# Layer 0's queries join the seven products; row sums kept in DRAM; two norms pinned

## The chip, the cores and the metric

The kernel runs on one core of a Trainium2 chip. A core has a matrix engine (TensorE, PE below; its weight loads are shown as PEld), a vector engine (VectorE, DVE), a scalar engine (ScalarE, ACT), a general-purpose engine (GpSimd, POOL) and a sync engine (SyncE, SP) that here only issues DMAs. The metric is device time in microseconds of one execution; the kernel before takes 2171.02 us, the median of three runs (2167.05 to 2172.69).

## The reference, cut to what matters

Two transformer layers in float32. Layer 0 is attention with 16 heads of 128 on 2048 tokens of width 512 (four sequences of 512), then a mixture of eight experts with two chosen per token; layer 1 is the other way round. The change is in the projections and rotations of layer 0's attention:

```python
q = (hidden_states @ Wq + bq).reshape(Bq, Sq, NH, D).transpose(0, 2, 1, 3)
q = apply_rope(rmsnorm(q, qn_w), pos)
...
ck = apply_rope(rmsnorm(entries @ Wk + bk, kn_w), block_ends)
sc = jnp.einsum('bhsd,bcd->bhsc', q, ck) * scale
...
lk = apply_rope(rmsnorm((hidden_states @ Wlk + blk).reshape(Bq, Sq, NH, D).transpose(0, 2, 1, 3), kn_w), pos)
lv = (hidden_states @ Wlv + blv).reshape(Bq, Sq, NH, D).transpose(0, 2, 1, 3)
```

`apply_rope` turns the first 64 of a head's 128 entries by the token's position and leaves the other 64 alone. `rmsnorm` divides by the root of the mean square and multiplies by a weight vector. Scores against compressed keys `ck` keep the eight largest per token; scores against `lk` are taken in a band of 128 tokens.

## The kernel before, in words

**Steps.** Layer 0's attention is done in 32 steps, one for each pair of heads (a group, `g`) and each sequence (`b`), in the loop at line 822. Step i computes the attention of its pair and, in between, the projections of step i+1, which `project(i+1)` hands over as pieces (lines 828 to 856). The written order within a step is: scores of the first head (`sp`, `st`, lines 600 and 609); queries of the first half of the tokens (`pq`, line 554); first keys; sums of rows; a job of other work (`run0`); scores of the second head; transposes `trs` of the first head's sparse weights (line 635); another job; second keys with the transposes `trq` (line 543) of what is ready; the first context (`ca`, `cb`, `cc`, lines 651 to 657); `trs` of the second head; queries of the second half; a job; the second context; transposes `trc` of the first context (line 677); a job; values; more `trq` and `trc`; the output product `op` (line 685), added to the residual (line 688).

**Jobs.** In the early steps they are layer norms of later sequences, compressed keys and routing; in steps 5 to 24 the experts of layer 0 (`trm`, line 382, then `hp`, line 392, with the weights fetched by POOL one expert ahead, lines 373 and 375); from step 25 on the experts' results are gathered and added, and layer 1's first norms are done.

**Seven products.** Tokens are cut into two halves and the 512 input features into two halves, and the weights for keys and for values are the two column blocks. Instead of eight block products, seven are computed of sums of blocks: p1, p2 (first keys, line 560), p6, p7, p4 (second keys, line 567), p5, p3 (values, line 578). They need sums of token blocks (`x1`, `x2`, `x3`; lines 515 to 518 and 571, DVE, each step) and sums of weight blocks (`combine_weights`, line 96, once per group). Each product is a PSUM bank of two chunks of 256 columns, four matmuls. Queries are computed directly: sixteen matmuls of 256 columns per step (line 550).

**After a product.** DVE adds partial results and biases on the way out of PSUM. `rope` (line 426) takes squares on ACT with a running sum, the power -1/2 on POOL (lines 434 to 437), and rotates on DVE, over all 128 entries of a head since the table `t1` also holds the norm's weight. Queries are then scaled by their norm on ACT (line 447); keys are not, their norm enters as the scale of the exponential (line 613). `trq` turns the result and ACT copies it to `qkT` (line 544), which has two buffers.

**The context.** `context` (line 640) uses three PSUM banks of the tag `sc`, which has three buffers; the second head's context takes the same three. They are free when DVE has read the sums (line 660), ACT has scaled the sparse half (line 668) and DVE has added both (line 670). Products, queries, `hp` and `op` share the tag `mm` with three banks, transposes the tag `tr` with two.

**Who orders the instructions.** The kernel is written as one program; a planner gives each engine a fixed order ahead of time. It goes by program order, but when by its own estimate an instruction could not start yet it takes a later one that could. Instructions wrapped in `keep_in_program_order` keep their written order among each other. On the chip each engine works through its list, and each queue of DMAs (SP's, ACT's and POOL's) through its own.

**The start.** SP loads the first token tile, `Wq` and the biases, then the second tile, `Wlk`, the norm vectors, the rotation tables, two more tiles, and `Wlv` (lines 119 to 139). `tables` (line 175) makes `t1` and `t2` on POOL from them. `layernorm` (line 197) takes statistics on DVE, the power on POOL and the result on DVE, then four transposes `trx`.

## Time and profile before

| | |
|---|---|
| median of three runs | 2171.02 us |
| the profiled execution | 2168.7 us |
| its span, first to last instruction | 2166.8 us |
| layer 0's attention loop | about 61 to 1500 us |
| layer 1 | about 1500 to 2167 us |
| PE busy | 2108.3 us, 97% of the span |
| PEld busy | 1392.0 us, 64% |
| DVE busy | 1458.9 us, 67% |
| ACT busy | 848.4 us, 39% |
| POOL busy | 687.0 us, 32% |
| DMA, mean over the span | 97 GB/s |

An engine's busy time is the union of its instructions. Matmul records overlap (their ends are modelled), so the time that a stream of matmuls takes is read from one start to the next. A float32 matmul is recorded as two instructions. The chain of work that ended last has PE with 68% of the span, DVE 8%, POOL 5%, DMA 3%, ACT 3%; 13% are issue. Its largest lines are 524 (the seven products, 15%), 554 (queries, 9%) and 685 (output product, 9%).

### The profile page before, as it was taken

The numbers are of one execution on the slowest core, as the hardware profiler recorded it, in microseconds if no ns is written. First come the engines' busy times: TensorE is split into PE (matmuls) and PEld (weight loads), VectorE is DVE, ScalarE is ACT, GpSimd is POOL, SyncE is SP. The second block draws the span as 40 slices with busy tenths as digits, with TensorE's granted clock in tenths as the row PEclk, the third lists the DMA queues.
The fourth block names the chain that finished last, engine by engine and source line by source line (L and its number), as shares of the span: only waits on it lengthen the run. The fifth ranks groups of instructions, "written<-read, shape, count | busy, mean of one in ns | idle before, by whom it ended". The sixth has DMA issues, their size and how long they took to land.

```text
span 2166.8 us, 28936 instructions
## 1 busy us (share of the span) xinstructions
PE 2108.3 (97%) x9970; PEld 1392.0 (64%) x9970; DVE 1458.9 (67%) x3674; ACT 848.4 (39%) x2649; POOL 687.0 (32%) x725
## 2 busy tenths in 40 slices
PE   6999999999999999999999999999999999999998
PEld 5667877777777777777777887885334343443332
DVE  6868976666666766666666788885485444446775
ACT  3444444334444334444433444552333233333332
POOL 3212234343323323333323444443012222213430
PEclk9999999999999999999999999999999999999998
DMA  7001023322322332232232112102016566653321
GB/s 229 35 11 38 11 73 97 106 78 83 105 98 74 105 105 71 83 124 80 78 123 83 59 50 63 35 30 92 10 69 209 203 227 209 205 198 117 107 83 41
DMA packets 70813, 211.24 MB, mean 97 GB/s; under 512 B 8449, under 2 KB 25857, under 8 KB 60673
## 3 DMA queue, kind: packets, MB, share of 16 engines
q0 software_dynamic: 22592, 139.47, 19.2%
q1 hardware_dynamic: 45760, 65.63, 9.4%
q10 hardware_dynamic: 2304, 4.20, 0.5%
q8 instruction: 81, 1.33, 0.3%
q14 instruction: 76, 0.61, 0.1%
HBM read 176.24 MB, written 33.03 MB: 97 GB/s over the span
## 4 chain that ended last, share of the span: by engine, by line
PE 68%; issue 13%; DVE 8%; POOL 5%; DMA 3%; ACT 3%; SPq 0%; POOLq 0%; ACTq 0%; DVEq 0%
PE p L524 15%; PE pq L554 9%; PE op L685 9%; PE hp_r L392 7%; PE st L609 4%; PE sp L600 2%; PE trq L543 2%; PE qp L905 2%; POOL we_r L375 2%; PE ca L653 2%; PE o L976 1%; DVE pS L936 1%; PE st L916 1%; DMA row_r<-yd,slot_r 1%; PE cc L657 1%
## 5 line engine op out<-in xcount | busy, mean ns | idle before, releaser
L392 PE MATMUL hp_r<-we_r,xT_r 128*128 128x512 f32 x624 | 283.4, 597 | 4.3 <-DMA we_r<-in_ewx,wrow_r 4.2
L617 POOL TENSOR_TENSOR lT<-lT,lmask 128x512 f32<-128x512 f32 (+1 forms) x128 | 151.2, 1196 | 318.6 <-ACT lT L613 318.6
L554 PE MATMUL pq<-Wq,xnT 128*128 128x256 f32 x1024 | 234.0, 381 | 1.2 <-DVE u L570 1.2
L685 PE MATMUL op<-Wo,cT 128*128 128x512 f32 x512 | 230.5, 599 | 2.1 <-DVE lv L587 2.1
L554 PEld LDWEIGHTS pq<-Wq,xnT 128*128 128x128 f32 x1024 | 190.2, 191 | 24.9 <-DVE u L570 1.5
L392 PEld LDWEIGHTS hp_r<-we_r,xT_r 128*128 128x128 f32 x624 | 115.1, 191 | 139.4 <-issue 129.6
L373 POOL DMA_INDIRECT xr_r<-xnd,rows_r x78 | 83.6, 1072 | 330.9 <-PE trm_r L382 232.9
L613 ACT ACTIVATE lT<-st,ss 128x256 f32<-128x256 f32 (+1 forms) x256 | 96.8, 443 | 234.2 <-PE st L609 234.1
L544 ACT COPY qkT<-trq 128x512 f32<-128x512 f32 x128 | 74.7, 583 | 231.6 <-PE trq L543 231.2
L685 PEld LDWEIGHTS op<-Wo,cT 128*128 128x128 f32 x512 | 91.7, 190 | 113.8 <-issue 82.3
L918 ACT ACTIVATE pT<-st 128x1024 f32<-128x1024 f32 x128 | 123.8, 1019 | 70.1 <-PE st L916 54.5
L437 POOL TENSOR_TENSOR ss<-ss,nhalf 128x4 f32<-128x4 f32 x128 | 144.5, 1129 | 10.7
L384 ACT COPY xT_r<-trm_r 128x512 f32<-128x512 f32 x78 | 45.2, 580 | 260.6 <-PE trm_r L382 203.0
L688 DVE TENSOR_TENSOR acc<-acc,op 128x512 f32<-128x512 f32 x128 | 87.5, 684 | 80.7 <-PE op L685 80.5
L394 DVE TENSOR_TENSOR yr_r<-hp_r,we_r 128x512 f32<-128x512 f32 x78 | 53.7, 688 | 116.5 <-PE hp_r L392 116.5
L447 ACT ACTIVATE r<-r,ss 128x128 f32<-128x128 f32 x256 | 81.9, 390 | 105.8 <-POOL ss L437 103.4
L524 PE MATMUL p<-Wlv,x 128*128 128x256 f32 x512 | 117.5, 380 | 0.0
L524 PE MATMUL p<-Wlk,xnT 128*128 128x256 f32 x512 | 117.4, 383 | 0.0
L524 PE MATMUL p<-wT,x 128*128 128x256 f32 x512 | 117.4, 380 | 0.0
L407 POOL DMA_INDIRECT row_r<-yd,slot_r x64 | 75.3, 1176 | 120.1 <-DVE row_r L1008 53.6
L524 PEld LDWEIGHTS p<-wT,x 128*128 128x128 f32 x512 | 95.9, 190 | 23.8 <-issue 12.1
L524 PEld LDWEIGHTS p<-Wlv,x 128*128 128x128 f32 x512 | 95.5, 190 | 20.7 <-issue 9.1
(253 smaller groups left out, 4394.4 us busy)
## 6 DMA issues: line engine op xcount, KB each, us to landing
yd<-yr_r SPq DMA_DIRECT2D x78, 256.0 KB, 2.4
acc<-in_x SPq DMA_DIRECT2D x16, 256.0 KB, 5.1
Wq<-in_Wq SPq DMA_DIRECT2D x8, 512.0 KB, 3.7
Wlk<-in_Wlk SPq DMA_DIRECT2D x8, 512.0 KB, 3.6
xnd<-xn ACTq DMA_DIRECT2D x16, 256.0 KB, 2.6
Wlv<-in_Wlv SPq DMA_DIRECT2D x8, 512.0 KB, 9.1
Wo<-in_Wo SPq DMA_DIRECT2D x8, 512.0 KB, 3.6
xnd<-xn SPq DMA_DIRECT2D x16, 256.0 KB, 2.0
```

The costliest lines, as they stand in the source:

```text
L373: G.indirect_dma_start(out=x, out_offset=None, in_=xnd, in_offset=at_rows(self.r.rows[:, i : i + 1]))
L392: PE.matmul(hp, lhsT=xT[:, k, :], rhs=w[:, ts(k, HID)], start=(k == 0), stop=(k == KC - 1))
L437: G.tensor_tensor(ss, ss, nhalf[:, 0:n], ALU.pow)
L447: A.activation(r1[:, h, :], r1[:, h, :], AF.Copy, scale=ss[:, h : h + 1])
L524: PE.matmul(p[:, c, :], lhsT=x[:, k, ts(c, P)], rhs=w[:, k, :], start=(k == 0), stop=(k == 1))
L554: PE.matmul(pq[:, c, :], lhsT=xnT[:, k, ds(b * S + (2 * t + c) * P, P)], rhs=w_q[:, k, :], start=(k == 0), stop=(k == KC - 1))
L609: PE.matmul(st[:, ds((t % 2) * 256, n)], lhsT=qkT[:, HG + h, ts(t, P)], rhs=qkT[:, h, ds(t * P, n)], start=True, stop=True)
L613: A.activation(lT[:, ds(half * 512 + c * 256, n)], st[:, ds(c * 256, n)], AF.Exp, scale=norm_k[(i, half)][:, c * HG + h : c * HG + h + 1])
L617: G.tensor_tensor(dst, dst, lmask.rearrange("p a w j -> p (a w j)")[:, 0:n], ALU.mult)
L685: PE.matmul(op, lhsT=cT[:, h, ts(t, P)], rhs=wo[:, h, :], start=(h == 0), stop=(h == HG - 1))
L688: V.tensor_tensor(acc[:, n, :], acc[:, n, :], op, ALU.add)
L918: A.activation(pt[:, ts(pair, 2), :], st, AF.Exp, scale=SCALE1)
```

## The change

The two column blocks of the seven products are no longer keys and values. Block A is now the pair's queries (256 columns) and the first head's keys (128); block B is the pair's values (256) and the second head's keys (128). The host lays the weights and biases out so (`wA`, `wB`, `bA`, `bB`). Each product has 384 columns and is made in two chunks, each with a PSUM bank and an eviction of its own. The separate query matmuls are gone.

With that: all of block A for the first half of the tokens comes out of `first` (p1, p2), for the second half out of `second` (p6, p7, p4), block B out of `third` (p5, p3). Keys of the first head are turned by `turn_keys(0)` late in the step, those of the second head, which stand in `lv` beside the values, by `turn_keys(1)` in the next step, after its first scores. `qkT` has one buffer. The rotation covers the 64 entries that turn and is done in place; what the norm weights do to the other 64 goes into a vector `turned` that scales keys on their copy out of PSUM. Tables have 64 entries for three heads, and the compressed keys have tables of their own.

The four sums of rows are computed in the first four projections only and written to DRAM (`xsd`); the later ones load them on SP. The first two token tiles are loaded ahead of the weights, the weights come in halves, and the statistics and results of the first two layer norms are pinned to program order. A constant that nothing used is dropped.

```diff
     def load_group(g, between=None):
...
+        b2 = wpool.tile([P, 2, 3 * D], F32, tag="b2", name=f"b2_{g}")
         ws = []
+        for i, nm in enumerate(("wA", "wB")):
+            w = wpool.tile([P, KC, 3 * D], F32, tag=nm, name=f"{nm}_{g}")
+            for f in range(2):
+                nc.sync.dma_start(out=w[:, ts(f, 2), :],
+                                  in_=a[nm][g, ts(f, 2 * P), :].rearrange("(k p) c -> p k c", p=P))
+                if between:
+                    between(nm, f)
+            nc.sync.dma_start(out=b2[:, i, :], in_=a["b" + nm[1]][g].partition_broadcast(P))
             ws.append(w)
...
+    def load_between(nm, f):
+        if nm == "wA" and f == 1:
+            for w, src in enumerate(("qn_w", "kn_w")):
+                nc.sync.dma_start(out=nw[:, w, :], in_=a[src].partition_broadcast(P))
+                nc.sync.dma_start(out=wcol[:, w : w + 1], in_=a[src].rearrange("(d o) -> d o", o=1))
+            nc.sync.dma_start(out=cos, in_=a["c_cos"][:, :, 0:R])
             nc.sync.dma_start(out=sin, in_=a["c_sin"])
             for n in range(2, TC):
                 load_x(n)
     load_x(0)
+    load_x(1)
     groups = {0: load_group(0, load_between)}
...
     def layernorm(n, pool, bank):
+        pin = tc.keep_in_program_order if n < 2 else (lambda x: x)
         st = small.tile([P, 6], F32, tag="st", name=f"st_{n}")
-        V.bn_stats(st, acc[:, n, :])
+        pin(V.bn_stats(st, acc[:, n, :]))
...
-        V.tensor_scalar(xn, acc[:, n, :], mv[:, 0:1], mv[:, 1:2], ALU.subtract, ALU.mult)
+        pin(V.tensor_scalar(xn, acc[:, n, :], mv[:, 0:1], mv[:, 1:2], ALU.subtract, ALU.mult))
...
+    def rotate(x, tt1, tt2, n, pool, name):
...
+        V.tensor_tensor(r1, x[:, :, 0:R], tt1, ALU.mult)
+        V.tensor_tensor(r2[:, :, 0:32], x[:, :, 32:R], tt2[:, :, 0:32], ALU.mult)
+        V.tensor_tensor(r2[:, :, 32:R], x[:, :, 0:32], tt2[:, :, 32:R], ALU.mult)
+        V.tensor_tensor(x[:, :, 0:R], r1, r2, ALU.add)
...
+    def load_sums(i):
+        for n in range(4):
+            xs[n] = wk0.tile([P, 2, 256], F32, tag=f"x{n}", name=f"x{n}_{i}", bufs=1)
+            if i >= B:
+                nc.sync.dma_start(out=xs[n].rearrange("p k t -> p (k t)"), in_=xsd[steps[i][1], n])
...
+        def product(nm, x, w, c):
+            p = psum("mm", f"{nm}_{i}_{c}")[:, 0 : 3 * D]
+            for k in range(2):
+                PE.matmul(p, lhsT=x[:, k, ts(c, P)], rhs=w[:, k, :], start=(k == 0), stop=(k == 1))
+            return p
...
+        def finish(t):
+            x = qb[t].rearrange("p c (h d) -> p (c h) d", d=D)
+            sq[t] = squares(x, 6, wk0, f"{i}_{t}", float(D))
...
+            rotate(x, by(t1), by(t2), 6, wk0, f"{i}_{t}")
+            for j in (0, 1, 3, 4):
+                A.activation(x[:, j, :], x[:, j, :], AF.Copy, scale=sq[t][:, j : j + 1])
...
+        def second(between):
+            u2, u3 = u["u2"], tmp("u3")
             t2_, t3_, t4_ = sums_w[g]
+            for c in range(2):
+                V.tensor_tensor(u2[:, c, :], product("p6", xs1, t2_, c), u2[:, c, :], ALU.add)
+                V.tensor_tensor(u3[:, c, :], product("p7", xs2, t3_, c), u2[:, c, :], ALU.add)
             between()
+            qb[1] = wk0.tile(rows3, F32, tag="qb", name=f"qb1_{i}")
+            for c in range(2):
+                V.tensor_tensor(qb[1][:, c, :], u3[:, c, :], product("p4", x22, t4_, c), ALU.subtract)
+            finish(1)
+        def third():
+            u2, u3 = u["u2"], u["u3"]
+            u5 = wk0.tile(rows3, F32, tag="qb", name=f"u5_{i}")
+            by_head = lambda x: x.rearrange("p c (h d) -> p c h d", d=D)
+            for c in range(2):
+                V.tensor_tensor(u5[:, c, :], product("p5", xs0, w_b[:, 0:2, :], c), b2[:, 1, :], ALU.add)
+            V.tensor_tensor(lv[:, 2:4, :, 0:D], by_head(u3), by_head(u5), ALU.add)
+            V.tensor_tensor(u2, u2, u5, ALU.add)
+            for c in range(2):
+                p3 = product("p3", xs3, w_b[:, 2:4, :], c).rearrange("p (h d) -> p h d", d=D)
+                V.tensor_tensor(lv[:, c, :, 0:D], p3, by_head(u2)[:, c], ALU.add)
+            x = lv[:, :, 2, 0:D]
+            ss = squares(x, TC, wk0, f"{i}_k", float(D))
+            rotate(x, t1[:, :, 2, :], t2[:, :, 2, :], TC, wk0, f"{i}_k")
...
     for i, (g, b) in enumerate(steps):
...
+        em0, lT0 = scores(i, 0, now)
+        turn_last(1)
+        if more:
+            load_sums(i + 1)
+            qkT, sums_x, first, second, third, turn_queries, turn_keys = project(i + 1)
+            first()
+            sums_x()
         run0((i, 0))
+        em1, lT1 = scores(i, 1, now)
         sT0 = turn(i, 0, em0)
         run0((i, 1))
-        back_k1 = keys_b(back_q0)
-        back_k0()
+        if more:
+            second(lambda: turn_queries(0))
         ctx0 = context(i, 0, lT0, sT0, lv)
         sT1 = turn(i, 1, em1)
-        back_q1 = queries_b()
         if b == 2 and g + 1 in groups:
             combine_weights(g + 1)
         run0((i, 2))
-        back_k1()
         ctx1 = context(i, 1, lT1, sT1, lv)
         turn_context(i, 0, ctx0, cT)
+        if more:
+            turn_queries(1)
         run0((i, 3))
-        values_()
-        back_q1()
+        if more:
+            turn_keys(0)
+            third()
         turn_context(i, 1, ctx1, cT)
```

## The prediction

> **What bounds the kernel now.** I read the slices first, then busy time by stage, then the timeline of one step engine by engine, then the waits of TensorE (PE), and the start last. The slices say PE is busy to nine tenths and at full clock from the second slice on. The stages say how hard that is: layer 0 has 32 steps, and a step with expert work is

> ```profile
> core 0: us, PE busy (x) PEld busy (x) DVE busy (x) ACT busy (x) POOL busy (x), PEclk, DMA share, GB/s
> 61.16:110.86 49.70, 46.13 (x249) 34.21 (x248) 38.81 (x120) 21.11 (x73) 13.84 (x20) 1.00 0.07 27
> 849.81:896.79 46.98, 46.98 (x237) 36.25 (x237) 30.36 (x84) 19.60 (x73) 14.65 (x16) 1.00 0.23 79
> 1267.00:1308.00 41.00, 40.10 (x217) 32.83 (x218) 36.13 (x93) 18.86 (x70) 18.45 (x20) 1.00 0.15 44
> ```

> (columns after the stretch: length, then busy us and instructions per engine.) From 520 to 1179 us PE waits for nobody; the steps repeat at 46.98 us. In the early steps and in steps 25 to 30 PE stands idle for up to 3.6 us per step. So in layer 0 PE's own work sets the time, and VectorE (DVE, 30 of 47), ScalarE (ACT, 20), GpSimd (POOL, 15) and the DMAs have slack. The same step on PE:

> ```profile
> 849.64 7.17 PE L685 MATMUL op<-Wo,cT 128*128 128x512 f32 x16
> 856.65 1.05 PE L600 MATMUL sp<-ckT,qkT 128*128 128x32 f32 x8
> 859.06 3.62 PE L554 MATMUL pq<-Wq,xnT 128*128 128x256 f32 x16
> 862.51 3.62 PE L524 MATMUL p<-Wlk,xnT 128*128 128x256 f32 x16
> ...
> 869.25 3.60 PE L392 MATMUL hp_r<-we_r,xT_r 128*128 128x512 f32 x8
> 872.69 3.62 PE L524 MATMUL p<-wT,x 128*128 128x256 f32 x16
> ...
> 880.75 0.61 PE L657 MATMUL cc<-cv,sT 128*128 128x129 f32 x4
> 881.20 0.60 PE L635 MATMUL trs<-ident,s 128*32 128x128 f32 x4
> 881.64 3.62 PE L554 MATMUL pq<-Wq,xnT 128*128 128x256 f32 x16
> 885.09 0.60 PE L382 MATMUL trm_r<-ident,xr_r 128*128 128x128 f32 x4
> 885.97 0.39 PE L653 MATMUL ca<-lv,lT 128*128 128x129 f32 x2
> ```

> Start to start is what counts. A matmul stands as two records. Sixteen records of 256 columns take 3.454 us (859.06 to 862.51 and on): 0.2159 each. Eight of 512 take 3.44 (869.25 to 872.69): 0.430; the sixteen of line 685 take 7.01: 0.438.

> **The matmuls.** Per projection, before: queries 32 records and seven products of 8, in all 88 x 0.2159 = 19.00 us. After: seven products x 2 halves x 2 chunks x 2 records = 56 records of 384 columns, a shape the trace lacks. Halfway between 0.2159 and 0.430 it costs 0.323, halfway to 0.438 it costs 0.327; I take 0.3235, nearest to the back-to-back rows. 56 x 0.3235 = 18.12, so **0.88 us less** (0.69 to 0.91). Transposes stay at 16 per step. Over 32 projections: **-28 us** (-22 to -29).

> [...] The rows show 0.84 ns per column at 256 and at 512 alike, so the rows decide and give nothing beyond the columns.

> **Evictions, rotation, row sums.** DVE rows: 0.69 us for 512 columns, 0.415 for 256, 0.283 for 128; by that line 384 is 0.55 and 768 about 0.95. Before, a projection takes 11 x 0.69 + four row sums x 0.68 + four rotations x 1.67 = 17.0 us. After: 14 x 0.55 + 2 x 0.95 = 9.6, two rotations of 384 and 192 columns (1.8 each) and one of 256 and 128 (1.4): 14.6, plus 2.7 while the sums are still made (the first four projections). DVE is not the bound in a 46.98 us step, so the 2.4 us are worth nothing there; without that cover they are worth 2.4. ACT keeps 16 squares, 8 scalings and 4 copies; POOL has three norm pairs instead of four. Products now come every 1.29 us against 0.55 of eviction, and three banks let PE run two ahead: the top-k of the first scores holds DVE until 862.35, PE needs the first bank back at 863.4, 0.5 us of room.

> **Sums from DRAM.** 28 steps load four tiles of 256 KB and four write them. Loads of that size land in 2.7 us (the xa rows of layer 1), four one after another 11 us. Their buffers come free when the products of the step before have read them, p3 as the last at about 849; p6 wants them at about 871. Even if all four are issued only then, they have 21 us. The wait they add stands on SP; behind it are the expert rows' writes (2.4 us to land) and the next group's weights, neither wanted for 14 us. Four issues at 0.43 us (SP's rows) are 1.7 us of SP. Price: 0; if all cover went, up to 11 us a step, which nothing in the trace points to. The expert weights land 6.4 us after their issue and have 14.9 us in the new order (16.2 now).

> **What is late next: the second context.** This is the step I trust least. Its banks are those of the first context, which are free only after sums, ACT's halves and DVE's last multiply-add. Today the second half of the queries (3.46 us, 881.64) lies between. It is gone: after 'cc' there is only trs 0.44 and trm 0.44 in steps 5 to 24, trs alone in most others. Now the engines that free the banks:

> ```profile
> 881.40 0.16 DVE L660 TENSOR_SCALAR sums<-cc 128x2 f32<-128x2 f32 x1 [0.28 <-PE cc L657]
> 882.82 0.86 DVE L670 SCALAR_TENSOR_TENSOR ctx<-ca,sums,half 128x128 f32<-128x128 f32 x3
> ```

> 'cc' ends at 881.2, 'ca' is free at 883.7: 2.5 us. PE would come after 0.88: a hole of **1.6 us**, if ACT takes the halves at once. For the second context it does not:

> ```profile
> 888.07 0.19 ACT L432 ACTIVATION_READ_ACCUMULATOR sq<-qb_q 128x1 f32 x1
> 889.74 1.28 ACT L447 ACTIVATE r<-r,ss 128x128 f32<-128x128 f32 x4 [1.48 <-POOL ss L437]
> 890.92 0.60 ACT L668 ACTIVATE half<-cb,sums 128x128 f32<-128x128 f32 x2
> ```

> The halves were ready at 889.0 and stood 1.9 us behind the scaling of the queries, which waited for POOL's power (1.04 us). Nobody noticed, for 7 us of matmuls followed. In the changed kernel the second half's queries come out of p4, right ahead of the first context: eviction 0.55, three squares 1.3, POOL 1.5, scaling 1.28 puts the scaling at about 3.7 us after p4 and the halves behind it at 5.0, 'ca' free 4.4 us after 'cc': a hole of 3.5 us. Against it: the order on PE is not strictly the written one. At 285 to 295 us op, trc, sp and st are interleaved record by record, so the planner fills holes that it sees, and p5 (2.59 us) needs only its row sum and a bank. What it does not see is POOL's delay: the wait 'PE trck <- ACT r_ck' (1.7 us, 1.7, 0.4) is such a case. Bounds per step: 0 (all filled) and 1.9 (3.5 less 1.6 filled). I take **0.45**, nearer to zero because in steady steps PE now shows no hole at all: x 31 = **+14 us** (0 to +59).

> **The start.**
> ```profile
> 11.34 2.11 PE L210 MATMUL trx<-ident,xn 128*128 128x128 f32 x8 [11.34 <-DVE xn L206]
> 13.32 5.09 PE L554 MATMUL pq<-Wq,xnT 128*128 128x256 f32 x16
> 21.75 0.66 PE L210 MATMUL trx<-ident,xn 128*128 128x128 f32 x4 [3.34 <-DVE mv L203]
> ```
> The first norm's result waited on DVE behind the second tile's statistics, which waited for its load (sixth in SP's queue, there at 9.7 us). Now x0 and x1 load first and the norms are pinned, so 'xn' can be done at about 6.0 (power at 5.37 plus 0.55), 5.3 us sooner. But the bias of the first products is queued behind both halves of the weights, the norm vectors, cos, sin and two tiles, 2.2 MB; at the first slice's 229 GB/s plus 2.9 us to land it comes at 12 to 15, against the first eviction at 23.55 today. From 23 to 61 DVE is full, so the gain ends between nothing and 9 us. Tables on POOL: 12 operations instead of 6, about 5.7 us against 5.2 (640 elements 1.58, 160 about 0.5), still ahead of the third and fourth norm's power. I take **-4** (-9 to +2).

> The new columns of single floats (two loads, 4 bytes per partition) resemble the 'part' load, which landed in 2.9 us, so I charge nothing. [...]

> **Sum.** -28 + 14 - 4 = -18 on the profiled execution, 2168.7 (span 2166.8 and 1.9 around it): 2150.7. The median of the three, 2171.0, lies 2.3 above: **2153**.

> **Rivals.** About 0.3% (6.5 us) is what a measurement of this kernel can tell from no change.
> (1) *All holes filled*: -28 - 6 = 2137. For it: interleaving at 285 us, no hole in steady steps. Against: planned times that POOL misses.
> (2) *The second context waits*: place, line 653's first matmul; price 1.9 a step. 31 x (1.9 - 0.88) = +32, less 4 + 1 for the start and the projection ahead of the loop: about 2198, **slower**. It decides from 0.88 us per step on. For it: 890.92 above. Against: p5 is ready.
> (3) *Saving given back*: hole of 0.7 to 1.1, 2165 to 2177, no change. The lower cover in steps 25 to 30 would do it there alone (today 4.9 us from the end of the second context to its transposes).
> (4) *Row sums late*: p6 waits on a load. Slower; against it the 11 us of four loads within 21.

> **Chances.** Forecast 0.37 (2145 to 2164), (1) 0.27, (2) 0.20, (3) 0.14, (4) 0.02. Faster 0.64, same 0.14, slower 0.22. The range for 8 in 10 takes in (1) and the lower part of (2): 2136 to 2186; the forecast's own is 2145 to 2164.

> **What would show it.** Right: a steady step near 46.5 us, records of 384 columns 0.32 apart, p5 ahead of the second 'ca', first transposes at 6 to 7 us. The hole shows as idle before 'ca' with DVE ctx or ACT as releaser. Wrong: 384 columns at over 0.34; PE waits for x or for 'u' evictions; steps over 46.98.

## The result, and the profile after

The changed kernel takes 2271.04 us (median of four, 2267.98 to 2271.81) against 2170.1 for the kernel before (median of four, 2167.05 to 2172.69): ratio 1.0463, 95% interval 1.0445 to 1.0481. It is **slower by 4.6%**, and the prediction was wrong in direction and range. The profiled execution spans 2269.7 us (2166.8 before) at a mean granted clock of 0.977 (0.993).

Stretches of the changed kernel first, an early step, a steady one and a late one, then two pieces inside the steady step (columns: length, then busy us and instructions of each engine, granted clock, DMA):

```profile
core 0: us, PE busy (x) PEld busy (x) DVE busy (x) ACT busy (x) POOL busy (x), PEclk, DMA share, GB/s
112.52:162.90 50.38, 48.34 (x231) 31.18 (x229) 37.49 (x107) 23.42 (x81) 11.51 (x12) 1.00 0.09 32
856.10:906.97 50.87, 47.79 (x206) 31.98 (x205) 29.87 (x80) 20.17 (x72) 14.52 (x14) 0.97 0.30 104
1306.52:1352.90 46.38, 41.69 (x182) 28.67 (x180) 30.61 (x87) 19.32 (x70) 17.63 (x18) 0.93 0.24 69
882.93:886.01 3.08, 0.00 (x2) 0.03 (x1) 0.50 (x2) 2.32 (x9) 1.80 (x2) 1.00 0.14 31
886.01:890.62 4.61, 4.61 (x27) 4.61 (x28) 1.23 (x7) 1.00 (x4) 0.00 (x0) 0.63 0.12 42
```

The steady step was 46.98 us with TensorE busy throughout. Now it is 50.87, TensorE stands idle for 3.08 of them, and in the 4.61 us behind the idle the mean granted clock is 0.63: for 3.41 us of them, from 886.88 on, TensorE runs at half clock (0.5). The same step on TensorE:

```profile
859.38 5.33 PE L538 MATMUL p<-wA,xnT 128*128 128x384 f32 x16
864.54 0.60 PE L392 MATMUL trm_r<-ident,xr_r 128*128 128x128 f32 x4
...
881.89 0.60 PE L650 MATMUL trs<-ident,s 128*32 128x128 f32 x4
882.33 0.60 PE L392 MATMUL trm_r<-ident,xr_r 128*128 128x128 f32 x4
886.01 0.46 PE L668 MATMUL ca<-lv,lT 128*128 128x129 f32 x2 [3.08 <-DVE ctx L685]
886.30 0.39 PE L666 MATMUL ca<-lv,lT 128*128 128x129 f32 x2
...
887.49 0.64 PE L666 MATMUL cb<-lv,lT 128*128 128x129 f32 x2
889.21 1.07 PE L672 MATMUL cc<-cv,sT 128*128 128x129 f32 x4
```

Sixteen records of 384 columns go from 859.38 to 864.54: 0.3225 each. Between the contexts stand trs and trm and nothing else, and `ca` of the second context waits. From 887.05 the same two-record pieces that took 0.22 us start to start take 0.43, until 890.3. What `ca` waited for, on GpSimd (POOL), ScalarE (ACT) and VectorE (DVE), in the timelines of the same step:

```profile
881.67 0.56 POOL L443 TENSOR_SCALAR ss<-ss 128x6 f32<-128x6 f32 x1 [8.16 <-ACT sq L442]
882.31 1.35 POOL L444 TENSOR_TENSOR ss<-ss,nhalf 128x6 f32<-128x6 f32 x1
...
883.69 1.28 ACT L552 ACTIVATE qb<-qb,ss 128x128 f32<-128x128 f32 x4 [2.12 <-POOL ss L444]
884.88 0.60 ACT L683 ACTIVATE half<-cb,sums 128x128 f32<-128x128 f32 x2
...
882.33 0.20 DVE L678 RECIPROCAL sums<-sums 128x8 f32<-128x8 f32 x1
885.51 0.35 DVE L685 SCALAR_TENSOR_TENSOR ctx<-cb,sums,half 128x128 f32<-128x128 f32 x1 [2.98 <-ACT half L683]
885.78 0.86 DVE L685 SCALAR_TENSOR_TENSOR ctx<-ca,sums,half 128x128 f32<-128x128 f32 x3
```

The halves (ScalarE's scaled copies of a context's sparse half) need only the reciprocal, done at 882.5. They start at 884.88, for on ScalarE's queue the scaling of the second half's queries stands ahead of them and waits for GpSimd's power until 883.69. The waits of TensorE over the whole execution (us in total, times, longest):

```profile
PE ca L668 <- DVE ctx L685: 68.6, 26, 3.4
PE p L538 <- DVE u L578: 14.6, 6, 3.3
PE trx L220 <- DVE xn L216: 12.7, 4, 5.9
...
PE trg_r L236 <- ACT lr_r L231: 4.1, 1, 4.1
```

Layer 0 carries all of it. Step by step (ends of line 700's matmuls, line 685 before), changed less before: +5.7 us in step 0, -0.1 in steps 1 to 4, **+70.7 in steps 5 to 23**, **+26.8 in steps 24 to 30**, +0.6 in step 31, and -0.9 in layer 1, whose code is the same.

Steps 5 to 23 are accounted for: 19 x (3.08 - 0.88) = 41.8 from the idle less the saved matmuls, and 16 stretches of 3.41 us at half clock, each taken at half its length, 1.7 (50.87 less 49.22 makes 1.65): 27.3. That is 69.1 of 70.7; the rest is that step 5 took only 45.2 before. A step takes 50.87 where the half clock follows its idle, and 49.22 where it does not (steps 8, 13, 18).

### The profile page after: what moved, and what is told of

It reads as the page before. It is cut to its first block, busy times and chain, and to the rows that moved or that the text cites. A ratio compares the mean times of both kernels' runs of the same rounds, so it can differ in the third digit from the quotient of the medians.

```text
span 2269.7 us, 27315 instructions
## 1 busy us (share of the span) xinstructions
PE 2120.4 (93%) x8946; PEld 1234.2 (54%) x8946; DVE 1444.4 (64%) x3596; ACT 867.5 (38%) x2649; POOL 673.8 (30%) x667
## 4 chain that ended last, share of the span: by engine, by line
PE 60%; issue 13%; DVE 9%; POOL 7%; ACT 6%; DMA 4%; SPq 0%; POOLq 0%; ACTq 0%; DVEq 0%
PE p L538 20%; PE op L700 10%; PE hp_r L402 6%; ACT sq L442 3%; PE st L624 3%; PE sp L615 2%; PE qp L922 2%; POOL ss L444 2%; DMA row_r<-yd,slot_r 2%; POOL we_r L385 2%; PE o L993 1%; ACT qb L552 1%; PE ca L668 1%; PE st L933 1%; DMA we_r<-in_ewx,wrow_r 1%
## 5 line engine op out<-in xcount | busy, mean ns | idle before, releaser
L538 PE MATMUL p<-wT,x 128*128 128x384 f32 x512 | 175.6, 493 | 4.5 <-DVE u L578 3.8
L538 PE MATMUL p<-wB,x 128*128 128x384 f32 x512 | 177.1, 489 | 0.3 <-DVE u L591 0.3
L538 PE MATMUL p<-wA,xnT 128*128 128x384 f32 x512 | 173.4, 491 | 2.2 <-DVE u L570 2.2
L442 ACT ACTIVATE sq<-qb 128x128 f32<-128x128 f32 x384 | 119.0, 310 | 125.4 <-DVE qb L583 57.7
L668 PE MATMUL ca<-lv,lT 128*128 128x129 f32 x384 | 83.4, 302 | 69.1 <-DVE ctx L685 68.6
L538 PEld LDWEIGHTS p<-wA,xnT 128*128 128x128 f32 x512 | 95.5, 192 | 63.6 <-DVE u L570 3.4
L443 POOL TENSOR_SCALAR ss<-ss 128x6 f32<-128x6 f32 x64 | 34.9, 546 | 291.2 <-ACT sq L442 291.2
L538 PEld LDWEIGHTS p<-wB,x 128*128 128x128 f32 x512 | 92.6, 191 | 52.3 <-DVE u L591 1.3
L552 ACT ACTIVATE qb<-qb,ss 128x128 f32<-128x128 f32 x256 | 81.8, 390 | 98.9 <-POOL ss L444 95.1
L628 ACT ACTIVATE lT<-st,ss 128x256 f32<-128x256 f32 (+1 forms) x128 | 47.1, 448 | 176.6 <-PE st L624 176.6
```

Of the source, the lines that this page charges most:

```text
L442: A.activation(sq, x[:, h, :], AF.Square, accum_out=ss[:, h : h + 1])
L538: PE.matmul(p, lhsT=x[:, k, ts(c, P)], rhs=w[:, k, :], start=(k == 0), stop=(k == 1))
L552: A.activation(x[:, j, :], x[:, j, :], AF.Copy, scale=sq[t][:, j : j + 1])
L668: PE.matmul(loc[t], lhsT=lT[:, ds(t * 256, P)], rhs=lv[:, t, h, :], start=(t == 0), stop=True)
```

## The experiments

Layer 1, untouched by every run, took between 664.2 and 672.1 us in the profiled executions, one of each kernel, with 19.5 to 33.7 us of it at half clock. The start varies too: in the changed kernel and the seven others that share its start, step 0's first scores come at 65.2 to 69.0 us. So a difference of a few us in a total says little; the lengths of like steps of layer 0 repeat to some 0.02 us within an execution, and they decide.

**The halves first.** Is the idle made by ScalarE's order? The last line below calls the scaling for t = 1, each instruction pinned in program order.

```diff
-            for j in (0, 1, 3, 4):
-                A.activation(x[:, j, :], x[:, j, :], AF.Copy, scale=sq[t][:, j : j + 1])
+            if t == 0 or i == 0:
+                scale(t, lambda ins: ins)
...
         ctx0 = context(i, 0, lT0, sT0, lv)
+        if more:
+            scale_last[i + 1]()
```

> Edit: the changed kernel with one thing moved: ScalarE's scaling of the second half's query rows (line 552, t = 1) comes behind the two copies of halves (line 683) of the first context, where it stood ahead of them and waited for GpSimd's power. Theory (the hole ahead of the second context is the scaling's wait for GpSimd, 2.3 us of the 3.1, and only an idle of that length is followed by 3.4 us of half clock): the first context's ca is read 0.4 us after its halves, at about 883.9 instead of 885.9 in the step at 856 us, the idle ahead of the second context falls to 1.2 to 1.6 us, no half clock follows it, and a step of 5 to 23 takes 47.3 to 47.8 us instead of 49.2 to 50.9: 2180 to 2195 us in all. Rival A (the hole is the bank itself and the chain of halves, sums and reciprocal, whatever ScalarE's order): the idle stays near 3 us and the time at 2270. Rival B (the half clock has another cause than the idle): the idle falls but the stretches at half clock stay, 2205 to 2220 us.

Measured: 2179.73 us (ratio to before 1.0051, 1.0033 to 1.0069), 91 us less than the changed kernel. Its timelines of VectorE (the reciprocal), ScalarE, VectorE again and TensorE in a steady step:

```profile
833.51 0.20 DVE L684 RECIPROCAL sums<-sums 128x8 f32<-128x8 f32 x1
...
833.81 0.62 ACT L689 ACTIVATE half<-cb,sums 128x128 f32<-128x128 f32 x2 [1.06 <-DVE sums L684]
834.33 0.62 ACT L689 ACTIVATE half<-cc,sums 128x128 f32<-128x128 f32 x2
834.87 1.28 ACT L557 ACTIVATE qb<-qb,ss 128x128 f32<-128x128 f32 x4
...
834.74 0.86 DVE L691 SCALAR_TENSOR_TENSOR ctx<-ca,sums,half 128x128 f32<-128x128 f32 x3
...
833.52 0.60 PE L392 MATMUL trm_r<-ident,xr_r 128*128 128x128 f32 x4
834.97 0.46 PE L674 MATMUL ca<-lv,lT 128*128 128x129 f32 x2 [0.85 <-POOL ss L444]
```

The halves start 0.1 us after the reciprocal (833.51 and 0.20), the idle is 0.85 us, no stretch at half clock is left in steps 5 to 23, and each from step 6 on takes 47.00 (step 5 46.5). The idle is shorter than the 1.2 to 1.6 expected, and so are the steps, and the total is 0.3 us under its band; both rivals fall. (The releaser printed for `ca`, GpSimd's power, frees no bank; in the code the bank comes free with the multiply-adds on VectorE, 834.74 here, so a printed releaser is checked against the timeline.) The matmuls' saving shows here too: 46.98 - 0.88 + 0.85 = 46.95.

**Work in the hole.** The idle stays where it is made, and ready matmuls are put into it.

```diff
-        run0((i, 1))
+        expert = 5 <= i < 24
+        if not expert:
+            run0((i, 1))
...
         sT1 = turn(i, 1, em1)
-        run0((i, 2))
+        run0((i, 1) if expert else (i, 2))
```

> Edit: the changed kernel in which, in steps 5 to 23, the first piece of the expert's products (3.4 us of matmuls that wait for nothing of this step) is emitted between the turn of the first context and the second context instead of ahead of it, and the two later pieces one place later each; ScalarE's order is as it was. Theory (TensorE is idle there only because the planner has nothing that is ready, and the half clock follows from the idle): the wait ahead of the second context disappears in those 19 steps, no stretch at half clock is left in them, each takes 46.1 to 46.8 us instead of 50.2 in the mean; steps 24 to 30 keep their +3.9 each: 2195 to 2210 us in all. Rival (the idle only moves to where the piece was taken from, since the chain through ScalarE and GpSimd sets the step): steps stay over 49 us, 2255 us or more.

Measured: 2199.83 us (1.0137, 1.0120 to 1.0154). Fourteen of steps 5 to 23 take 46.60, five 47.2 to 47.7, more than was said: in those TensorE waits 0.5 to 1.1 us elsewhere, in three of them for an expert's weights. None of the nineteen has the wait ahead of the second context or a stretch at half clock, and steps 24 to 30 keep their loss (4.2 us each). The longer chain through ScalarE and GpSimd costs little where 3.4 us of matmuls lie over it (46.60 against 46.31 in a later run that has the halves first as well): the cover was what the change had removed.

**Dead work in the hole.** Two runs part the idle from the half clock that follows it, the first with seven matmuls in every step, the second with three and in steps 5 to 23 only.

```diff
+        if more:
+            idle = psum("mm", f"idle_{i}")
+            for _ in range(7):
+                tc.keep_in_program_order(PE.matmul(idle[:, 0:256], lhsT=ident, rhs=xnT[:, 0, 0:256], start=True, stop=True))
         ctx1 = context(i, 1, lT1, sT1, lv)
```

> Edit: the changed kernel with seven more matmuls of 256 columns ahead of the second context in every step with a projection, some 3.0 us in 14 records, whose result nothing reads. It does more work than the changed kernel and takes none away; no wait is removed. Theory (part of the loss is 3.4 us at half clock that follows an idle of 3.1 us, worth 1.7 us in about three of four steps): the idle is filled with dead work, the clock stays whole, every step of 5 to 23 takes 49.1 to 49.4 us, and the time falls by 20 to 40 us, to 2230 to 2250 us, with more matmuls. Rival (no effect of the idle on the clock, or the clock falls for its own reasons): stretches at half clock stay and the time is 2268 to 2285 us.

Measured: 2270.23 us (1.0459, 1.0440 to 1.0477). The total missed the 2230 to 2250, though steps 5 to 23 took 49.21 to 49.23 us, all nineteen, without half clock. What those steps won, 26 us, went elsewhere: by the end of step 4 the run is 14.4 us behind the changed kernel, and steps 24 to 31 lose another 10. There the dead matmuls stand in steps that had less idle to fill (none ahead of the second context in steps 0 to 4, 0.5 to 3.4 us in steps 24 to 30). The total alone would have told against a theory that the steps bear out, so the edit was cut to the steps in question and to a shorter filling:

> Edit: the changed kernel with three more matmuls of 256 columns, some 1.3 us in six records, whose result nothing reads, ahead of the second context in steps 5 to 23 alone. In the run with seven in all steps these 19 steps took 49.22 us each with no half clock, but the dead work held up the other steps. Theory (how long the idle lasts decides whether the half clock follows, and 1.8 us of it are too short): the second context starts no earlier than in the changed kernel, but no stretch at half clock is left in steps 5 to 23, all take 49.1 to 49.3 us, and the time is 2271 less 26, 2240 to 2250 us, with more work and no wait removed. Rival (a shorter idle draws the half clock too): steps stay at 50.9 in most and the time is 2262 us or more.

Measured: 2246.64 us (1.0358, 1.0341 to 1.0375), in the expected band. One step of it and the stretch after its idle, by stretches, and the idle on TensorE:

```profile
842.26:891.48 49.22, 47.45 (x211) 31.36 (x210) 29.85 (x80) 20.16 (x72) 14.52 (x14) 1.00 0.31 108
872.17:876.80 4.63, 4.63 (x33) 3.97 (x34) 2.04 (x10) 2.39 (x9) 0.00 (x0) 1.00 0.11 42
```

```profile
868.49 0.60 PE L392 MATMUL trm_r<-ident,xr_r 128*128 128x128 f32 x4
868.93 1.46 PE L865 MATMUL idle<-xnT,ident 128*128 128x256 f32 x6
872.17 0.46 PE L668 MATMUL ca<-lv,lT 128*128 128x129 f32 x2 [1.77 <-DVE ctx L685]
```

`ca` waits for the same row as before, 1.77 us instead of 3.08 because 1.3 us are filled, the clock stays at 1.00, and the step is 49.22 instead of 50.87. Nothing starts earlier; only the clock differs. So the kernel gets 24 us faster by 114 records of work whose result nobody reads: the half clock is a cost of its own, and in these steps how long the idle lasts decides whether it comes (behind 3.08 us in 16 of the 19, behind 1.77 in none).

**The kernel before, without its cover.** The other way round: nothing of the change, only the projection between the contexts moved ahead of the first one.

```diff
+        back_q1 = queries_b()
         ctx0 = context(i, 0, lT0, sT0, lv)
         sT1 = turn(i, 1, em1)
-        back_q1 = queries_b()
```

> Edit: the kernel before with one line moved: the products of the second half's queries (a projection of its own, 3.4 us and more of matmuls) are emitted ahead of the first context instead of between it and the second one. Same matmuls, same rows sums, no sums from DRAM. Theory (what the change lost is the cover between the two contexts, not its wider products nor its sums from DRAM): an idle of 3 to 4 us opens ahead of the second context, the half clock follows it in most steps, steps of 5 to 23 take 50 to 52 us instead of 46.98, and the time is 2250 to 2300 us. Rival (the wider products with their one bank for 384 columns, or the sums from DRAM, cost the time): 2165 to 2185 us.

Measured: 2282.35 us (1.0517, 1.0500 to 1.0535). Its timeline of TensorE has the same idle ahead of the second context, and by stretch its steps are 51.9 or 53.2 us:

```profile
857.29 0.77 PE L653 MATMUL ca<-lv,lT 128*128 128x129 f32 x2 [3.05 <-DVE ctx L670]
```

```profile
824.76:877.96 53.20, 50.15 (x237) 39.27 (x236) 30.46 (x83) 19.84 (x72) 14.53 (x16) 0.94 0.20 70
877.96:929.88 51.92, 48.87 (x238) 37.98 (x236) 30.47 (x83) 19.84 (x72) 14.53 (x16) 0.97 0.24 81
```

This is the change's loss without the change: no product of 384 columns, no sum from DRAM, and 113 us more. In the 53.20 us step the clock of 0.94 makes some 6.4 us at half clock, in the 51.92 us step 0.97 makes some 3.1 (both estimates); the longer stretch was not expected. Steps 24 to 30, however, lose only 5.5 us together here, where the changed kernel loses 26.8, although `ca` waits as long in them (9.7 us in all, 10.0 in the changed kernel). So those need another cause.

**The late steps.** With the halves first they still lose 14.8 us. VectorE's waits there (1180 to 1490 us of that run), and TensorE's from 1231 to 1488:

```profile
DVE acc L716 <- DMA row_r<-yd,slot_r: 16.3, 12, 3.7
...
PE p L538 <- DVE u L583: 9.8, 6, 3.3
```

An addition of gathered expert rows (line 716) stands on VectorE and waits for its gather, and the evictions of the products' banks stand behind it. Three runs, each from the kernel with the halves first:

The late adds:

```diff
-        run0((i, 1))
+        if i < 24:
+            run0((i, 1))
         if more:
             second(lambda: turn_queries(0))
+        if i >= 24:
+            run0((i, 1))
```

No sums from DRAM:

```diff
-            if i >= B:
-                nc.sync.dma_start(out=xs[n].rearrange("p k t -> p (k t)"), in_=xsd[steps[i][1], n])
...
-            if i < B:
-                V.tensor_tensor(xs[2], x11, x21, ALU.subtract)
+            V.tensor_tensor(xs[2], x11, x21, ALU.subtract)
...
```

The early adds, with the loads kept:

```diff
         turn_last(1)
+        if i >= 24:
+            run0((i, 0))
         if more:
             load_sums(i + 1)
...
             sums_x()
-        run0((i, 0))
+        if i < 24:
+            run0((i, 0))
```

> Edit: the kernel with the halves first (2180 us), in which the second of the four places for side work in steps 24 to 30 (an addition of gathered expert rows on VectorE, and the next gather) comes behind the second half's query products instead of ahead of them. Theory for the 2.2 us that these seven steps still lose each: the change put only some 4 us of work between the first and the second of these places, the addition waits in VectorE's order for rows that are gathered once the addition before it has freed their buffer (waits of 17.0 us on the gather in the stretch, 1.5 before the change), and the evictions of the products' banks stand behind it (TensorE waits 9.8 us for line 583 there). Moved, the wait goes: 1 to 2 us in each of seven steps, 2166 to 2174 us in all, steps 5 to 23 unchanged at 47.0. Rival (the loads of the sums from DRAM delay the gathers, or VectorE has too much work in these steps): 2177 to 2185 us.

Measured: 2184.19 us (1.0069, 1.0050 to 1.0088). A miss, and the rival's number: moving the second place later leaves 13.7 us of waits for gathers, TensorE now waits 9.3 us for a copy of ScalarE instead, and steps 24 to 30 still lose 12.7. The place was the wrong one.

> Edit: the kernel with the halves first (2180 us), in which the four sums of rows are computed by VectorE in every step, as steps 0 to 3 do, and no copy of them goes to DRAM or comes from it. Theory (as predicted, loading the sums from DRAM costs nothing where the clock and the second context are out of the way): steps 5 to 23 within 0.2 us of 47.00, 2174 to 2186 us in all; the four more VectorE instructions may cost up to 0.5 us a step in steps 24 to 30. Rival (the loads hold something up, the gathers of the expert rows above all): steps 24 to 30 get 1 to 2 us shorter each, 2164 to 2172 us.

Measured: 2167.42 us (0.9989, 0.9978 to 1.0001), the rival's number. Steps 24 to 30 lose nothing (-2.8 us), the waits for gathers fall to 3.2 us; steps 5 to 23 are 47.08 against 47.00, so there the loads are worth 0.08 us a step and cost nothing. (Step 4 takes 51.5 us here against 46.5, with 6.8 us at half clock, so the total shows less than steps 24 to 30 gain.) But the times of the additions give another reading than traffic. In the run with loads the first addition of step 25 starts 11.6 us into the step, its gather at 15.6, and the second addition waits 3.7 us at 20.4. Without the loads the first one starts at 1.8. It is pinned in program order, and in the two traces it comes after the VectorE work that is written just before it: with the sums on VectorE that is an early sum; with the sums in DRAM it is the rotation of the first queries (the rotation's last instruction starts at 1237.09, the addition at 1237.55). The next run keeps the loads and moves only that place:

> Edit: the kernel with the halves first (2180 us, sums still loaded from DRAM), in which the first of the four places for side work in steps 24 to 30 stands ahead of the next step's first query products instead of behind them. Theory (the run without the loads was 12 us faster not because the loads cost anything, but because an addition of gathered rows is pinned behind the VectorE instruction traced just before it: with the sums on VectorE that was an early sum, at 1.8 us of a step, and without them it is the rotation of the first queries, at 11.6 us; its gather and the next addition then come late, and the banks' evictions stand behind that addition): the waits of additions on gathers fall from 16.3 to under 6 us, steps 24 to 30 together from 303.8 to 288 to 293 us, 2164 to 2172 us in all, with the loads in place. Rival (the loads' traffic delays the gathers): steps 24 to 30 stay at 300 us or more, 2175 to 2185 us.

Measured: 2166.97 us (0.9986, 0.9977 to 0.9995). VectorE's wait in the same stretch:

```profile
DVE acc L716 <- DMA row_r<-yd,slot_r: 3.3, 5, 1.3
```

Steps 24 to 30 take 287.3 us (303.8 with the halves first, 289.0 before), with all the loads in place. So the loads' traffic is no cause, and the place of the additions is. That they lost their place together with the four sums on VectorE is read from the order in the traces; no run put another instruction where the sums had been.

**The start.**

```diff
-        V.memset(turned, 1.0)
-        V.tensor_scalar(turned[R:P, :], wcol[R:P, 0:1], wcol[R:P, 1:2], ...)
+        tc.keep_in_program_order(V.memset(turned, 1.0))
+        tc.keep_in_program_order(V.tensor_scalar(turned[R:P, :], wcol[R:P, 0:1], wcol[R:P, 1:2], ...))
...
     start_sequence(1)
+    start_sequence(2)
+    start_sequence(3)
     tables()
     first()
-    start_sequence(2)
-    start_sequence(3)
...
     first_logits(0)
+    scale_last[0](0)
...
```

> Edit: the kernel with the halves first (2180 us), with another order at the start: the two instructions for the turned keys' scale are pinned behind the first two norms, norms 2 and 3 stand ahead of the rotation tables (so that their powers do not wait for some 5 us of table work on GpSimd), and ScalarE's scaling of the first queries stands behind the copy of the first logits. Theory (the start lost what the pinned norms gained to these three orders: the second norm came 2.7 us late behind a load of key-norm weights, evictions 2 to 3 us late behind norms 2 and 3, and TensorE waited 4.1 us for the copy of the logits): step 0 ends 4 to 8 us earlier, 2172 to 2177 us in all. Rival (the start is bound by its loads): within 1.5 us of 2180.

Measured: 2179.02 us (1.0048, 1.0031 to 1.0064) against 2179.73: outside the band, and by its total the rival's. Yet step 0 ends 6.8 us earlier than with the halves first, as expected, and layer 0 still ends 6.8 us earlier. Layer 1 then took 669.6 us in the profiled execution against 664.2, with 33.7 us at half clock against 24.5, which makes 4.6 of the 5.4. So the three orders are worth what was said at the start; why layer 1 meets the clock differently was not tried.

**All together.** First with the late adds, then with the early ones (halves first, expert piece in the hole in steps 5 to 23, the new start):

> Edit: the halves first, the first expert piece between the two contexts in steps 5 to 23, the additions of gathered rows later in steps 24 to 30, and the new order at the start, all together. Theory (the wider products are worth 0.88 us a step as predicted, once nothing of the step waits): steps 5 to 23 at 46.1 to 46.3 us, 24 to 30 within 1 us of the kernel before, the start 2 to 6 us better: 2145 to 2162 us, faster than both kernels. Rival (each fix only moves the wait): 2168 us or more.

Measured: 2162.5 us (0.9964, 0.9950 to 0.9978), a half us above the band: most of steps 5 to 23 at 46.3, but the late steps lose 13.0 us.

> Edit: the halves first, the first expert piece between the two contexts in steps 5 to 23, the new order at the start, and in steps 24 to 30 the first place for side work ahead of the products. Theory: steps 5 to 23 at 46.0 to 46.4 us as in the run of all fixes before (46.3), steps 24 to 30 within 3 us together of the kernel before, the start 2 to 6 us better: 2146 to 2157 us. Rival (the late steps are not cured by the place): 2160 us or more.

Measured: **2147.7 us** (2147.18 to 2148.9; 0.9898, 0.9882 to 0.9913), 1.0% faster than the kernel before and 123 us below the changed one. A steady step of it by stretch:

```profile
795.13:841.45 46.32, 46.27 (x205) 30.12 (x204) 29.58 (x80) 20.50 (x72) 14.73 (x14) 1.00 0.34 114
```

TensorE is busy throughout again, in 46.3 us where it was 46.98; layer 0 ends 20.2 us before the old one, 9.5 of them won by the end of step 4 and 10.5 in steps 5 to 23. Those are less than the matmuls' 0.88 a step: most of these steps are 0.67 us shorter than before, four are 0.99, and step 14 took 47.97, in which TensorE waits 1.7 us for an expert's weights. What takes the other 0.2 us was not tried.

**A product in the hole.** In place of the expert piece and the moved scaling, the seventh product (p4, 2.6 us) between the contexts in every step, with the second half's transposes one job later. The early adds stay, and of the new start all but the moved scaling:

```diff
             between()
+
+        def fourth():
             qb[1] = wk0.tile(rows3, F32, tag="qb", name=f"qb1_{i}")
...
         sT1 = turn(i, 1, em1)
+        if more:
+            fourth()
...
         turn_context(i, 0, ctx0, cT)
+        run0((i, 3))
         if more:
             turn_queries(1)
-        run0((i, 3))
-        if more:
             turn_keys(0)
             third()
```

> Edit: the changed kernel with the seventh product's matmuls (the last of the second half's queries, 2.6 us of TensorE, with squares and scaling) between the two contexts in every step, where the kernel before had a projection of 3.4 us; side work of steps 24 to 30 ahead of the products, norms 2 and 3 ahead of the tables, turned keys' scale pinned; ScalarE's order else as in the changed kernel. Theory (2.6 us of matmuls in the hole leave at most some 0.5 us idle, too little for a stretch at half clock, and the scaling that the halves stood behind now comes after them by itself): steps 5 to 23 at 46.1 to 46.6 us, no half clock in them, steps 24 to 30 near the kernel before: 2142 to 2157 us. Rival (the wait moves to the second half's transposition, whose rows now come 6 us later): steps 47.0 to 48.5 us, 2165 to 2190 us.

Measured: 2169.89 us (1.0001, 0.9992 to 1.0010). Most of steps 5 to 23 at 46.64 without half clock, a little above the band's edge; the late steps lose 7.5 us, and TensorE waits 12.7 us in all for the scaled second half's queries. Neither side was right as a whole: the hole is closed, and a part of the wait has moved to the transposition, as the rival had it. The profiled execution is the fastest of the eleven (2162.88), so where the others lose some 7 us more isn't shown.

## Why the prediction was wrong, step by step

**The matmuls: right.** 0.3235 us a record was said, 0.3225 is measured. The products of a step take 18.07 us from start to start with the halves first (18.12 said), against 19.00. That is 0.84 ns a column and record, as at 256 and 512: the wider products gain nothing beyond their columns.

**Evictions and row sums: right where they were hidden.** 384 columns took 0.56 us, 768 took 0.96, and VectorE bounds no steady step.

**Sums from DRAM, price 0: right for the loads, wrong for what left with them.** No product waits for a load. But the prediction looked only at what the four loads add, not at what is hung on the four VectorE instructions that go: the side work's first addition, pinned in program order, follows them. Without them it comes 9.8 us later in step 25 (11.6 against 1.8). The late place is worth 16.5 us in steps 24 to 30 (303.8 against 287.3).

**The second context, +14: here it failed.** The place, the chain and its rank were named: halves behind the scaling behind GpSimd's power, a hole of 3.5 us; 3.08 is measured. What failed is the step from 3.5 to 0.45, "the planner fills holes that it sees". The upper bound failed with it: 1.9 already takes 1.6 us of the 3.5 as filled and does not say with what; unfilled, its own chain gave 31 x 3.5 = 108 us instead of 59. The planner filled nothing in steps 5 to 23: trs, trm and then `ca`, with p5 written behind it. The evidence taken for filling (interleaving at 285 us, no hole in steady steps) came from a kernel that had 3.46 us of matmuls written into this very place. Why the planner left the hole open was not tried. That the order alone closes it, all but 0.85 us with the halves first and wholly with the expert piece or p4, is shown three ways.

**A term that was missing.** The sum had no term for the clock, though the prediction's own table showed it at 1.00 in steady steps. Layer 0 has 81.9 us at half clock (3.4 before); if TensorE was busy throughout, that costs (81.9 - 3.4)/2, some 39 us, an estimate. Rival (2) was the mechanism, priced at 1.9 us a step; 3.08 and 1.7 in five steps of six make 4.5.

**The start, -4: wrong by 12.** The first transposes came at 5.88 us (6 to 7 said). The second ones did not follow:

```profile
5.88 1.11 PE L220 MATMUL trx<-ident,xn 128*128 128x128 f32 x4 [5.88 <-DVE xn L216]
11.63 1.11 PE L220 MATMUL trx<-ident,xn 128*128 128x128 f32 x4 [4.64 <-DVE xn L216]
...
31.07 0.59 PE L236 MATMUL trg_r<-ident,lr_r 9*128 9x9 f32 x4 [4.08 <-ACT lr_r L231]
```

On VectorE `turned` (line 191) stood between the second norm's statistics and its aggregate, waiting 3.32 us for the small key-norm columns, which the prediction had charged with nothing. The first scores of step 0 show what the start lost: before, in the changed kernel, and with the three orders changed:

```profile
61.16 1.16 PE L600 MATMUL sp<-ckT,qkT 128*128 128x32 f32 x8
69.04 1.05 PE L615 MATMUL sp<-ckT,qkT 128*128 128x32 f32 x8
55.94 1.16 PE L621 MATMUL sp<-ckT,qkT 128*128 128x32 f32 x8
```

The start is 7.9 us longer in the profiled executions (4.1 to 7.9 in the eight that share it; the kernel before without its cover, whose start is the old one, has its first scores at 63.2), and step 0 itself is 2.2 us shorter, which leaves the 5.7. With the three orders changed the scores come 5.2 us earlier than before: the gain that was forecast was there, behind these orders.

**Added up.** Term by term, in us over layer 0: matmuls -30 (0.93 x 32; said -28), `ca`'s waits +68.6 and half clock some +39 (said +14 for both), start +7.9 (said -4), late additions +16.5 (said 0). That makes +102 of the +103.7, but the terms overlap: 6.8 us of the added half clock lie in the start, and the 16.5, measured between two other kernels, holds a stretch of 6.8 us of it. So the near match of the sum proves nothing by itself; the count by steps and the runs do. By them steps 5 to 23 lose 70.7, the idle and its half clock; steps 24 to 30 lose 26.8, of which the halves first take away 12 and the early adds the rest.

## What to carry to other kernels

Before work is taken out from between two pieces, list the chain that ran under it on the other engines: the gap is what that chain still needs, and the order on those engines sets it, not the amount of work (here a scaling ahead of the halves: 3.08 us idle, and 0.85 with the halves first). Do not count on a planner to fill a gap unless the trace shows it filling that one. An instruction that goes takes its place in the order with it, so look for what is written and pinned behind it.

## What the runs showed of the hardware

The cut between 0.42 and 0.45 holds for these steps alone. Elsewhere in the traces falls follow busier stretches, one of 0.53 in the start of the changed kernel (the fall at 50.61) and one of 0.53 in layer 1 of the kernel before (at 2132.39), and one of 0.22 in the start of the changed kernel (6.24 to 9.65) has no fall behind it. So how busy TensorE must be to keep the clock isn't settled by these runs.
